# A layered kernel with two mixtures of experts: the second mixture's rows are sorted sequence by sequence, in groups of five and three

## The chip, the cores and the metric

The kernel runs on one core of a Trainium2 chip. The metric is device time in microseconds (us). Five engines work side by side, each through its own queue in order: PE multiplies matrices, DVE and ACT do elementwise work, POOL does some of it and issues the indirect DMAs, SP issues the other DMAs. PE weight loads appear as a track of their own, PEld.

## The reference, cut to what matters

```python
# x: 8 sequences of 512 rows of 128, float32
x = x + 0.5 * moe(layernorm(x))        # layer 0: 8 experts, top 2, 128 -> 512 -> 128
x = x + attention(layernorm(x))        # layer 1: 16 heads of 8, causal, with rope
x = x + 0.5 * moe(layernorm(x))        # layer 2: same weights as layer 0
x = x + 0.5 * fp6_linear(layernorm(x)) # block quantized, block 32
x = x + mix(layernorm(x))              # rmsnorm, gates, causal scan, gated MLP
x = x + 0.5 * fp6_linear(layernorm(x))

def moe(u):
    logits = u @ router_w + router_b
    gates, idx = top_2(logits); gates = softmax(gates)
    return sum(gates[k] * (relu(u @ W1[idx[k]] + b1[idx[k]]) @ W2[idx[k]] + b2[idx[k]]) for k in (0, 1))
```

## The kernel before, in words

The eight sequences X[b] stay in SBUF, four blocks of 128 rows each. A mixture layer works in two groups of sequences (`GROUPS`; layer 0: three and five, layer 2, the third layer, four and four). For each group there are three stages.

`moe_front` (L336) routes. Each sequence, once the layer before has finished it (`done`), is normalized and scored. When all of the group are scored, one set of operations over all its rows finds the two experts of each row (`first_of_max`), counts rows by expert with two matrix products (L435, L436), and computes each row's place in a table in which every expert starts at a multiple of 256 rows. Then 8 indirect DMAs per sequence (L496) scatter the normalized rows into `rows_in[g]` in DRAM, one generator step each.

`moe_tiles` (L505) takes the table in tiles of 256 rows, `tiles_of(n)` = 4n + 7 for n sequences. `load` reads the tile's expert number into a register of SP (L514), and loads that expert's weights `wx` (L516) and the rows `xs` (L520); the latter depends on every scatter of the group. `rows_turned` transposes the rows (L530), `first` does the first product (L544) and the relu (L552, L554), `second` the second (L564), adds a bias (L572) and stores into `rows_out` (L576). `ahead` loads five tiles ahead and turns up to two ahead, as soon as the loads are emitted. A tile takes four generator steps. The loop emits `first(i, half)` and then `second(i - 1, half)`, so the end of a tile is emitted after the start of the next one.

`moe_combine` (L608) gathers the two result rows of every row (L636, 8 indirect DMAs per sequence on POOL) and adds them to X with the gates (L627). The first sequence is finished after 14 gathers.

All code is emitted in program order by generators. `drive(main, (side, rate), ...)` takes `rate` steps of each side per step of the main one; so the order of work on every engine's queue is the order of these steps, and the rates set what stands between what. `attention` (L652) takes 10 steps before its loop over t and then two for every t; it works through the sequences in order and finishes sequence b with L836. `tails` (L1041) runs the last three layers of the sequences, each 27 steps (`fp6`, `mix`, `fp6`), a new one every 8 steps, at most four at once. The end of the order reads:

```python
drive(
    attention(list(range(nb)), 1),
    (early, 1.0), (tiles, 2.2), (gathering, 0.8), (third, 1.0), (fourth, 1.0), (beside, 0.9),
)
finish(third)
drive(until(beside, lambda: filled(2, 0)), (fourth, 1.5))
rest = tails(GROUPS[2][0] + GROUPS[2][1])
drive(beside, (fourth, 1.5), (moe_combine(2, 0), 1.0), (rest, 0.33))
drive(rest, (moe_combine(2, 1), 2.0))
```

Here `third` and `fourth` route the groups of layer 2, `beside` is its tiles, `sent(s, g)` is true once the group's scatters are all emitted, `filled(s, g)` once its tiles' stores are. `early`, `tiles` and `gathering` are what is left of layer 0.

Of the kernel before, what the change touches and what calls it, by code (L numbers as in the profile page):

```python
# [25 lines left out]
NGF = 3  # L26
TW = 256

GROUPS = {0: [[0, 1, 2], [3, 4, 5, 6, 7]], 2: [[0, 1, 2, 3], [4, 5, 6, 7]]}
SIZES = sorted({len(g) for gs in GROUPS.values() for g in gs})  # L30
GTX = SIZES[-1] * NT


def tiles_of(n):

    return 2 * n * S // TW + NE - 1
# [7 lines left out]

NWIDE = 12
KBUFS = 5
AHEAD = 4


# [15 lines left out]
def drive(main, *sides):  # L65

    due = [0.0] * len(sides)
    for _ in main:
        for i, (g, rate) in enumerate(sides):
            due[i] += rate  # L70
            while due[i] >= 1.0:
                due[i] -= 1.0
                next(g, None)
# [12 lines left out]
def kernel(  # L86
# [71 lines left out]
        rows_in.append(dram.tile([n, P], F32, tag=f"rows_in{g}", name=f"rows_in{g}"))  # L158
        rows_out.append(dram.tile([n, P], F32, tag=f"rows_out{g}", name=f"rows_out{g}"))

    def clear_rows(g):
        n = rows_in[g].shape[0]
        nc.sync.dma_start(
            out=rows_in[g].rearrange("(n p) c -> p n c", p=P),
            in_=zero.unsqueeze(1).to_broadcast([P, n // P, P]),
        )

    for b in range(3, nb):
        load_x(b)
# [65 lines left out]
    def power(v, eps, name):  # L235
        rs = small.tile([P, NT], F32, tag="rs", name=f"rs_{name}")
        nc.vector.tensor_scalar_add(rs, v, eps)  # L237
        nc.gpsimd.tensor_tensor(rs, rs, mhalf[:, 0:NT], ALU.pow)  # L238
        return rs

    def moments(src, name, mv=None):
        st = small.tile([P, NT, nc.vector.BN_STATS_DIM], F32, tag="bst", name=f"st_{name}")
        if mv is None:
            mv = small.tile([P, NT, nc.vector.BN_AGGR_DIM], F32, tag="bmv", name=f"mv_{name}")
        for t in range(NT):
            nc.vector.bn_stats(out=st[:, t, :], in_=src[:, t, :])  # L246
        for t in range(NT):
            nc.vector.bn_aggr(out=mv[:, t, :], in_=st[:, t, :])
        return mv

    def normed_act(src, mv, rs, name, tag="u"):

        nb_ = small.tile([P, NT], F32, tag="nbias", name=f"nb_{tag}_{name}")
        nc.vector.scalar_tensor_tensor(nb_, mv[:, :, 0], -1.0, rs, ALU.mult, ALU.mult)  # L254
        u = wk.tile([P, NT, P], F32, tag=tag, name=f"{tag}_{name}", bufs={"um": 5, "row": 4}.get(tag, 2))
        for t in range(NT):
            nc.scalar.activation(  # L257
                u[:, t, :], src[:, t, :], AF.Identity,
                scale=rs[:, t : t + 1], bias=nb_[:, t : t + 1],
            )  # L260
        return u

    def normed(src, mv, rs, name):

        u = wk.tile([P, NT, P], F32, tag="um", name=f"um_{name}", bufs=5)
        for t in range(NT):
            nc.vector.tensor_scalar(
                u[:, t, :], src[:, t, :], mv[:, t, 0:1], rs[:, t : t + 1],
                ALU.subtract, ALU.mult,
            )  # L270
        return u

    def by_feature(src, name, scale=None, tag="uT"):

        tp = turned(src, name)
        ut = wk.tile([P, S], F32, tag=tag, name=f"uT_{name}")
        if scale is None:
            nc.scalar.copy(ut, tp)
        else:
            nc.scalar.activation(ut, tp, AF.Copy, scale=scale)  # L280
        return ut
# [35 lines left out]
        return ins  # L317

    def filled(s, g):
        return len(groups[s, g]["stored"]) == tiles_of(len(GROUPS[s][g]))  # L320

    def sent(s, g):
        return (s, g) in groups and len(groups[s, g]["scattered"]) == 2 * NT * len(GROUPS[s][g])

    groups = {}
    fronts = {}
    done = set()
    backlog = []
# [7 lines left out]
    def moe_front(s, g):  # L336
# [149 lines left out]
        nc.vector.tensor_tensor(g1[:, 1, :], ex, g1[:, 0, :], ALU.mult)  # L486
        yield

        scattered = []
        groups[s, g] = dict(at=at, gates=g1, eid=eid, scattered=scattered, stored=[])  # L490
        yield
        for n in range(len(bs)):
            for k in range(2):
                for t in range(NT):
# [7 lines left out]
                    scattered.append(unordered(ins, f"out{name}"))  # L502
                    yield

    def moe_tiles(s):  # L505

        order = [(g, i) for g in range(2) for i in range(tiles_of(len(GROUPS[s][g])))]
# [2 lines left out]
        def load(at):  # L510
            g, i = order[at]
            name = f"{s}_{g}_{i}"
            state = groups[s, g]
            e = nc.sync.value_load(state["eid"][0:1, i : i + 1], min_val=0, max_val=NE - 1)  # L514
            wx = wide(f"wx_{name}")
            nc.sync.dma_start(  # L516
                out=wx, in_=wexp[bass.ds(e, 1), :, :].rearrange("o p c -> p (o c)")
            )
            xs = wk.tile([P, 2, P], F32, tag="xs", name=f"xs_{name}", bufs=4)
            ins = nc.sync.dma_start(  # L520
                out=xs, in_=rows_in[g][ts(i, TW), :].rearrange("(h p) c -> p h c", p=P)
            )
            data_from(ins, state["scattered"])
            T[at] = dict(wx=wx, xs=xs, name=name, to=(g, i))

        def rows_turned(i):
            t = T[i]
# [51 lines left out]
            del T[i]  # L579

        n = len(order)
        loaded = turns = 0

        def ahead(i, turn):

            nonlocal loaded, turns
            while loaded < min(i + AHEAD + 1, n) and sent(s, order[loaded][0]):
                load(loaded)
                loaded += 1
            while turn and turns < min(i + 3, loaded):  # L590
                rows_turned(turns)
                turns += 1

        for i in range(n + 1):
            for half in range(2):
                if i < n:
                    ahead(i, turns <= i)
                    while turns <= i:
                        yield
                        ahead(i, True)  # L600
                    first(i, half)
                    ahead(i, half == 1)
                yield
                if i >= 1:
                    second(i - 1, half)
                    yield

    def moe_combine(s, g):  # L608

# [447 lines left out]
    def behind(gen, ready):  # L1057
        while not ready():
            yield
        yield from gen  # L1060

    def until(gen, ready):
        for _ in gen:
            yield
            if ready():
                return

    for s in GROUPS:
        for g in range(2):
            fronts[s, g] = moe_front(s, g)  # L1070
    first_front, second_front = fronts[0, 0], fronts[0, 1]
    next(first_front)
    next(second_front)
# [12 lines left out]
    )  # L1086
    backlog += [early, tiles, late]
    gathering = behind(late, lambda: filled(0, 1))
    third, fourth = fronts[2, 0], behind(fronts[2, 1], lambda: sent(2, 0))
    more_tiles = moe_tiles(2)  # L1090
    beside = behind(more_tiles, lambda: sent(2, 0))
    drive(
        attention(list(range(nb)), 1),
        (early, 1.0), (tiles, 2.2), (gathering, 0.8), (third, 1.0), (fourth, 1.0), (beside, 0.9),
    )
    finish(third)
    drive(until(beside, lambda: filled(2, 0)), (fourth, 1.5))
    rest = tails(GROUPS[2][0] + GROUPS[2][1])
    drive(beside, (fourth, 1.5), (moe_combine(2, 0), 1.0), (rest, 0.33))
    drive(rest, (moe_combine(2, 1), 2.0))  # L1100


# [75 lines left out]
```

## Time and profile before

| | us |
|---|---|
| median of 3 runs (1143.15 to 1146.67) | 1144.25 |
| the profiled execution, its own time | 1143.83 |
| its span | 1142.1 |
| PE busy | 947.7 (83%) |
| DVE busy | 674.8 (59%) |
| POOL busy | 539.0 (47%) |
| ACT busy | 485.0 (42%) |
| first L836 (a sequence leaves attention), last | 340.7, 715.8 |
| scatters of group 0 of layer 2 end; of group 1 | 607, 778 |
| last tile's L572 | 926.6 |
| gathers of group 0 of layer 2 begin; of group 1 | 795.9, 930.1 |

The span is the time between the first and the last instruction of the profiled execution; its own time is 1.7 us more. Busy times of the engines overlap. The page also cuts the span in 40 slices and gives the busy share of each; the trace can be asked for the busy times in any stretch, the instructions in order of time, and what each waited for (in square brackets: the idle time before it and what ended it).

### The profile page before, as it was taken

The numbers are of one execution on the slowest core, as the hardware profiler recorded it, in microseconds if no ns is written. First come the engines' busy times: TensorE is split into PE (matmuls) and PEld (weight loads), VectorE is DVE, ScalarE is ACT, GpSimd is POOL, SyncE is SP. The second block draws the span as 40 slices with busy tenths as digits, with TensorE's granted clock in tenths as the row PEclk, the third lists the DMA queues.
The fourth block names the chain that finished last, engine by engine and source line by source line (L and its number), as shares of the span: only waits on it lengthen the run. The fifth ranks groups of instructions, "written<-read, shape, count | busy, mean of one in ns | idle before, by whom it ended". The sixth has DMA issues, their size and how long they took to land.

```text
span 1142.1 us, 20198 instructions
## 1 busy us (share of the span) xinstructions
PE 947.7 (83%) x6681; PEld 651.5 (57%) x6681; DVE 674.8 (59%) x2484; ACT 485.0 (42%) x1063; POOL 539.0 (47%) x694
## 2 busy tenths in 40 slices
PE   3569989999999999999994999985779975367773
PEld 2459987777644445454442666875767753234432
DVE  7323244555688888779863641621566676877763
ACT  1323323324555566665552554321245444244441
POOL 3778063002487754433893221172852258754431
PEclk9999999999999999999997999997889986677787
DMA  9579776442110000000014213575655111000000
GB/s 294 176 243 276 227 219 190 148 126 68 29 27 24 25 13 1 1 2 2 29 57 144 60 62 95 160 224 175 200 173 173 47 33 41 23 19 10 10 10 18
DMA packets 88312, 110.05 MB, mean 96 GB/s; under 512 B 9360, under 2 KB 69648, under 8 KB 88208
## 3 DMA queue, kind: packets, MB, share of 16 engines
q1 hardware_dynamic: 80016, 91.97, 26.4%
q0 software_dynamic: 8192, 16.79, 4.9%
q8 instruction: 53, 0.87, 0.3%
q14 instruction: 51, 0.42, 0.1%
HBM read 79.63 MB, written 29.10 MB: 95 GB/s over the span
## 4 chain that ended last, share of the span: by engine, by line
PE 58%; DVE 16%; POOL 9%; issue 9%; ACT 4%; DMA 4%; SPq 0%; POOLq 0%; DVEq 0%; ACTq 0%
PE sa L731 11%; PE yp L564 10%; PE hp L544 10%; PE av L796 6%; PE sb L731 4%; POOL rows_in L496 3%; POOL y L636 3%; DVE seen L748 2%; DVE st L246 2%; ACT um L257 2%; PE lp L350 1%; PE gt L1015 1%; PE up L1016 1%; PE tp L231 1%; DMA xs<-rows_in 1%
## 5 line engine op out<-in xcount | busy, mean ns | idle before, releaser
L748 DVE CUSTOM_DVE_ANT_0 seen<-sa,future_s 128x128 f32<-128x128 f32 (+3 forms) x512 | 225.8, 487 | 91.6 <-PE sb L731 73.6
L777 ACT ACTIVATE pm<-sb 128x512 f32<-128x512 f32 (+1 forms) x384 | 180.5, 523 | 150.6 <-PE sb L731 138.8
L552 ACT ACTIVATE hs<-hp,wx 128x256 f32<-128x256 f32 x276 | 119.7, 470 | 255.3 <-PE hp L544 180.0
L731 PE MATMUL sb<-qa,ka 32*128 32x384 f32 (+3 forms) x1024 | 216.2, 468 | 0.7 <-DVE nstat L748 0.7
L564 PE MATMUL yp<-wx,hs 128*128 128x128 f32 x1472 | 202.9, 282 | 4.6 <-ACT hs L552 4.0
L564 PEld LDWEIGHTS yp<-wx,hs 128*128 128x128 f32 x1472 | 190.9, 197 | 19.0 <-issue 7.9
L544 PE MATMUL hp<-xt,wx 128*128 128x256 f32 x736 | 199.1, 395 | 0.0
L731 PE MATMUL sa<-ka,qz 32*128 32x256 f32 (+3 forms) x1024 | 197.2, 466 | 1.8 <-issue 1.6
L782 POOL TENSOR_SCALAR_AFFINE_SELECT pm<-pm 128x256 f32<-128x256 f32 x256 | 101.8, 411 | 191.2 <-ACT pm L777 190.3
L636 POOL DMA_INDIRECT y<-rows_out,at x128 | 131.9, 1030 | 85.8 <-DMA rows_out<-yo 50.4
L554 DVE TENSOR_SCALAR hs<-hp,wx 128x256 f32<-128x256 f32 x92 | 44.4, 483 | 171.8 <-ACT hs L552 161.9
L544 PEld LDWEIGHTS hp<-xt,wx 128*128 128x128 f32 x736 | 131.8, 198 | 24.3 <-issue 5.5
L731 PEld LDWEIGHTS sa<-ka,qz 32*128 32x128 f32 x1024 | 94.5, 184 | 75.0 <-issue 28.6
L731 PEld LDWEIGHTS sb<-qa,ka 32*128 32x128 f32 x1024 | 103.1, 184 | 16.0 <-DVE nstat L748 4.3
L496 POOL DMA_INDIRECT rows_in<-um,at x88 | 86.8, 986 | 45.8 <-DVE q L467 23.9
L796 PE MATMUL av<-pm,vpad 128*32 128x512 f32 (+3 forms) x1024 | 88.8, 442 | 2.6 <-DVE nstat L748 1.6
L238 POOL TENSOR_TENSOR rs<-rs,mhalf 128x4 f32<-128x4 f32 x35 | 36.2, 1033 | 87.6 <-DVE rs L237 87.5
L530 PE MATMUL xp<-cst,xs 128*128 128x128 f32 x184 | 37.3, 287 | 44.6 <-DMA xs<-rows_in 44.6
L231 PE MATMUL tp_xd<-cst,q 128*128 128x128 f32 x64 | 14.6, 370 | 63.8 <-POOL q L918 63.8
L257 ACT ACTIVATE um<-x,nb_um,rs 128x128 f32<-128x128 f32 x96 | 39.5, 482 | 63.5 <-DVE nb_um L254 55.5
L796 PEld LDWEIGHTS av<-pm,vpad 128*32 128x32 f32 x1024 | 23.5, 108 | 73.6 <-issue 43.9
L627 DVE SCALAR_TENSOR_TENSOR x<-y,g,x 128x128 f32<-128x128 f32 x128 | 54.0, 424 | 12.4 <-DMA y<-rows_out,at 10.2
(190 smaller groups left out, 1274.4 us busy)
## 6 DMA issues: line engine op xcount, KB each, us to landing
wx<-in_wexp SPq DMA_DIRECT2D x92, 578.0 KB, 3.9
xs<-rows_in SPq DMA_DIRECT2D x92, 128.0 KB, 4.1
rows_out<-yo SPq DMA_DIRECT2D x92, 128.0 KB, 1.9
rows_in<-zero SPq DMA_DIRECT2D x1, 3456.0 KB
rows_in<-zero SPq DMA_DIRECT2D x1, 2944.0 KB
x<-in_x SPq DMA_DIRECT2D x8, 256.0 KB, 5.4
y<-rows_out,at POOLq DMA_INDIRECT x128
out_x<-x SPq DMA_DIRECT2D x8, 256.0 KB, 2.0
```

Source lines behind the costliest of these rows:

```text
L257: nc.scalar.activation(u[:, t, :], src[:, t, :], AF.Identity, scale=rs[:, t : t + 1], bias=nb_[:, t : t + 1],)
L496: ins = nc.gpsimd.indirect_dma_start(out=rows_in[g][0 : NTL * TW, :], out_offset=bass.IndirectOffsetOnAxis(ap=at[:, k, i : i + 1], axis=0) ...
L544: nc.tensor.matmul(hp[:, k, :], wx[:, E_W1 + fc * P : E_W1 + (fc + 1) * P], t["xt"], start=True, stop=True,)
L552: nc.scalar.activation(hs[:, fc, :], hp[:, k, :], AF.Relu, bias=bias)
L564: nc.tensor.matmul(yp[:, h, :], t["hs"][:, fc, ts(h, P)], wx[:, E_W2 + fc * P : E_W2 + (fc + 1) * P], start=(fc == 0), stop=(fc == NFC - 1),)
L627: nc.vector.scalar_tensor_tensor(X[b][:, t, :], y[:, k, :], gates[:, k, i : i + 1], X[b][:, t, :], ALU.mult, ALU.add,)
L636: ins = nc.gpsimd.indirect_dma_start(out=y[:, k, :], out_offset=None, in_=rows_out[g][0 : NTL * TW, :], in_offset=bass.IndirectOffsetOnAxi ...
L731: nc.tensor.matmul(sc[:, at : at + hi - lo], stat[rows, ts(m, P)], mov[rows, lo:hi], start=True, stop=stop,)
L748: nc.vector.tensor_tensor_reduce(out=seen(w), in0=sc[:, at : at + w], in1=future_s[:, S - w : S], scale=-1.0, scalar=3.0e38, op0=ALU.add, ...
L777: nc.scalar.activation(pm[:, h % 2, 0:w], sc[:, 0:w], AF.Exp, scale=scale)
L782: nc.gpsimd.affine_select(out=dg, in_=dg, pattern=[[0, 2], [1, P]], compare_op=ALU.is_ge, fill=0.0, base=0, channel_multiplier=-1,)
L796: nc.tensor.matmul(av[32 * j : 32 * j + 32, m * P :], Q[b]["v"][:, m * NH + NR * j + r, :], U[n]["pms"][p, j // 2][:, j % 2, at : at + S - ...
```

## The change

For layer 2 `moe_stream` replaces `moe_front`. Each expert gets a stretch of a new table (`by_stretch`) that is long enough for all rows of the group, so that a sequence's places need only the counts of the sequences before it (`end`). Each sequence is routed by itself when attention has finished it, and its rows are scattered at once: with a generator step per scatter, but for the group's last sequence, whose eight scatters are emitted together. Where the tiles lie is known at the end; the first row of each is computed into `row`, and `load` reads it into a second register of SP for the address of `xs`. The places of the results in `rows_out` are then computed by adding `move`; `placed` tells that this has been done. The new tables are cleared beside attention by 16 DMAs. A tile's rows are turned `LANDING` = 6 steps after their load at the earliest. The groups of layer 2 are of five and three sequences (27 and 19 tiles; 23 and 23 before), and the rates of the order are others. `um` tiles have four buffers instead of five, and `rows_in[0]` has 27 tiles instead of 23.

```diff
-GROUPS = {0: [[0, 1, 2], [3, 4, 5, 6, 7]], 2: [[0, 1, 2, 3], [4, 5, 6, 7]]}
+GROUPS = {0: [[0, 1, 2], [3, 4, 5, 6, 7]], 2: [[0, 1, 2, 3, 4], [5, 6, 7]]}
...
+LANDING = 6
...
+    stretch = [len(bs) * S for bs in GROUPS[2]]
+    by_stretch = [
+        dram.tile([NE * n, P], F32, tag=f"by_stretch{g}", name=f"by_stretch{g}")
+        for g, n in enumerate(stretch)
+    ]
+
+    def clear_stretches():
+        for g, n in enumerate(stretch):
+            for e in range(NE):
+                cleared(by_stretch[g][ts(e, n), :])
+                yield
...
     def filled(s, g):
-        return len(groups[s, g]["stored"]) == tiles_of(len(GROUPS[s][g]))
+        return (s, g) in placed and len(groups[s, g]["stored"]) == tiles_of(len(GROUPS[s][g]))
...
+    def moe_stream(s, g):
...
+        for n, b in enumerate(bs):
+            while (s - 1, b) not in done:
+                yield
+            sl = ts(n, NT)
+            mv = moments(X[b], f"{s}_{b}")
+            rs = power(mv[:, :, 1], 1e-5, f"{s}_{b}")
+            yield
+            yield
+            yield
+            u = normed_act(X[b], mv, rs, f"{s}_{b}", tag="um")
...
+            lp = bank(f"lp_{s}_{b}")
+            for t in range(NT):
+                nc.tensor.matmul(lp[:, ts(t, NE)], ut[:, ts(t, P)], rw_s, start=True, stop=True)
+            yield
...
+            for k in range(2):
+                m = small_tile(f"m{k}", n, (NT, 1))
+                nc.vector.tensor_reduce(m, l, AX.X, ALU.max)
+                is_max = small_tile("k", n)
+                nc.vector.tensor_tensor(is_max, l, m.to_broadcast([P, NT, NE]), ALU.is_equal)
+                yield
...
+            nc.tensor.matmul(in_tile, before, by_expert, start=True, stop=True)
+            nc.tensor.matmul(
+                of_tile.rearrange("p (e t) -> p e t", e=NE), ones, by_expert, start=True, stop=True
+            )
+            yield
...
+            nc.vector.tensor_tensor(
+                place, place, end.unsqueeze(2).to_broadcast([P, NE, NT]), ALU.add
+            )
...
+            nc.vector.tensor_tensor(new_end, end, inc[:, :, NT - 1], ALU.add)
+            end = new_end
+            yield
+            for k in range(2):
+                for t in range(NT):
+                    ins = nc.gpsimd.indirect_dma_start(
+                        out=table,
+                        out_offset=bass.IndirectOffsetOnAxis(ap=at[:, k, t : t + 1], axis=0),
+                        in_=u[:, t, :], in_offset=None,
+                        bounds_check=NE * cap - 1, oob_is_err=False,
+                    )
+                    scattered.append(unordered(ins, f"out{name}"))
+                    if n < len(bs) - 1:
+                        yield
...
+        groups[s, g] = dict(
+            at=at, gates=g1, eid=eid, row=row, table=table, scattered=scattered, stored=[]
+        )
+        yield
...
+        placed.add((s, g))
...
-            ins = nc.sync.dma_start(
-                out=xs, in_=rows_in[g][ts(i, TW), :].rearrange("(h p) c -> p h c", p=P)
-            )
+            if "row" in state:
+                r = nc.sync.value_load(
+                    state["row"][0:1, i : i + 1], min_val=0, max_val=NE * stretch[g] - TW
+                )
+                rows = state["table"][bass.ds(r, TW), :]
+            else:
+                rows = rows_in[g][ts(i, TW), :]
+            ins = nc.sync.dma_start(out=xs, in_=rows.rearrange("(h p) c -> p h c", p=P))
             data_from(ins, state["scattered"])
-            T[at] = dict(wx=wx, xs=xs, name=name, to=(g, i))
+            T[at] = dict(wx=wx, xs=xs, name=name, to=(g, i), since=steps)
...
-            while turn and turns < min(i + 3, loaded):
+            while turn and turns < min(i + 3, loaded) and steps >= T[turns]["since"] + LANDING:
                 rows_turned(turns)
                 turns += 1
...
-            fronts[s, g] = moe_front(s, g)
+            fronts[s, g] = (moe_front if s == 0 else moe_stream)(s, g)
...
-    third, fourth = fronts[2, 0], behind(fronts[2, 1], lambda: sent(2, 0))
+    third, fourth = fronts[2, 0], behind(fronts[2, 1], lambda: (2, 0) in placed)
     more_tiles = moe_tiles(2)
     beside = behind(more_tiles, lambda: sent(2, 0))
+    back = behind(moe_combine(2, 0), lambda: filled(2, 0))
     drive(
         attention(list(range(nb)), 1),
-        (early, 1.0), (tiles, 2.2), (gathering, 0.8), (third, 1.0), (fourth, 1.0), (beside, 0.9),
+        (early, 1.0), (tiles, 2.2), (gathering, 0.8), (clear_stretches(), 0.2),
+        (third, 1.5), (fourth, 1.5), (beside, 2.0), (back, 0.8),
     )
     finish(third)
-    drive(until(beside, lambda: filled(2, 0)), (fourth, 1.5))
+    drive(until(beside, lambda: filled(2, 0)), (fourth, 2.0))
     rest = tails(GROUPS[2][0] + GROUPS[2][1])
-    drive(beside, (fourth, 1.5), (moe_combine(2, 0), 1.0), (rest, 0.33))
+    drive(beside, (fourth, 2.0), (back, 1.0), (rest, 0.6))
     drive(rest, (moe_combine(2, 1), 2.0))
```

## The prediction

> **What bounds the kernel now.** I read the page's slices first, then the busy time by stretch, then the chain that ended last, and last the instructions around the two largest holes of PE.
>
> ```profile
> PE   3569989999999999999994999985779975367773
> DVE  7323244555688888779863641621566676877763
> ```
>
> A digit is 28.6 us. PE (counting slices from 0) is full from slice 6 to 26 but for slice 21, near 610 us; it dips at slice 27, from 771 us, and from slice 32 (914 us) on it is not full again. So three places matter to this change: two holes, and the end.
>
> ```profile
> 600.00:625.00 25.00, 10.59 (x70) 5.39 (x68) 7.76 (x39) 4.89 (x12) 9.57 (x14) 0.66 0.50 164
> ...
> 766.00:783.00 17.00, 0.49 (x3) 0.52 (x4) 0.48 (x1) 0.18 (x1) 9.84 (x11) 0.58 0.19 55
> 783.00:817.00 34.00, 33.34 (x221) 30.53 (x220) 13.39 (x43) 9.18 (x21) 15.62 (x16) 0.96 0.83 249
> 817.00:927.00 110.00, 93.33 (x554) 78.34 (x555) 69.45 (x224) 53.42 (x122) 46.12 (x44) 0.92 0.40 118
> 927.00:1006.00 79.00, 43.56 (x167) 26.30 (x166) 56.99 (x169) 27.07 (x60) 59.29 (x56) 0.74 0.13 35
> 1006.00:1070.00 64.00, 44.75 (x160) 28.32 (x159) 46.34 (x150) 30.21 (x66) 28.54 (x26) 0.71 0.03 10
> 1070.00:1142.00 72.00, 39.66 (x173) 24.82 (x172) 40.78 (x116) 22.29 (x47) 21.85 (x20) 0.78 0.04 15
> ```
>
> Columns: stretch, its length, busy us of PE, PEld, DVE, ACT, POOL, then PE's clock, DMA share, GB/s. PE loses 14.4 us in the first row and 16.5 in the second. From 817 to 927 (tiles of group 1 with the first tails) PE is 85% busy: that stretch is PE's. From 927 (tails alone) no engine is over 76%: chains of short steps set it, 215 us long.
>
> ```profile
> 611.65 0.66 PE L530 MATMUL xp<-cst,xs 128*128 128x128 f32 x2 [9.00 <-DMA xs<-rows_in]
> 782.51 0.66 PE L530 MATMUL xp<-cst,xs 128*128 128x128 f32 x2 [16.84 <-DMA xs<-rows_in]
> 715.80 0.68 DVE L836 TENSOR_TENSOR x<-x,y 128x512 f32<-128x512 f32 x1
> 738.25 1.07 POOL L496 DMA_INDIRECT rows_in<-um,at  x1 [19.30 <-DVE q L467]
> 777.91 0.97 POOL L496 DMA_INDIRECT rows_in<-um,at  x1 [0.30 <-issue]
> ```
>
> Both holes are the same wait: the transpose of a group's first tile needs rows whose scatter has just ended. The last three rows give the second one: attention ends at 715.8, routing takes 22.4 us, 32 scatters 1.28 us apart take 40.6, and PE goes on at 783.2.
>
> [...]the last scatter lands 2.26 us after its issue (the chain's DMA row at 777.91), and SP issues xs at 780.30. [...]here L514's TENSOR_LOAD has a median of 273 ns, so I use that. [...]L352, of that size, takes 180 to 193.
>
> **When things happen in the new order.** I count yields. Attention has 10 before its loop and 2 per t; sequence b is done at yield 24b+57. DVE's L836 puts b=4 at 544.9, b=5 at 592.0, b=6 at 668.4, b=7 at 715.8: 47.1 us per 24 yields without tiles, 1.96 each. A tile in the dense stretch costs PE 3.73 us (L572 every 3.73). Taking the stall and 3.6 tiles (13.4) out of yields 177 to 201 leaves 48.7 us, and 5.4 tiles (20.1) out of 201 to 225 leaves 27.2.
>
> *Group 0 sent.* Sequence 4 is done at yield 153; 15 steps at rate 1.5 put its 8 scatters at yield 163 (564.5 us) and `sent` at 165. Eight scatters by 1.28 make 10.2, landing 2.3, xs 5.4 (the chain's row at 612.8): rows in at 582.4. LANDING lets the transpose go at yield 168, where PE arrives at 574: a stall of 8 instead of 14.4. The burst also sits ahead of the affine selects on POOL; I take that wait as inside the 8 (0 to 4 outside).
>
> *Attention's end.* Two tile steps per yield from 168 make 108 by yield 222, all 27 first halves. So 26.5 tiles lie inside attention where 9.3 do now. 582.4 + 17.6 + 48.7 + 27.2 + 26.5 x 3.73 (98.8) = 774.7, and 3 for the stream's waits (below): 778.
>
> *The new hole.* No tile is left to hide what follows. Routing of sequence 7 uncovered, from the rows at 715.8 to 723: 7.4 us to the logits, then 22 DVE operations of about 0.2 with two PE products between, together 14.7. Eight scatters 9.9, landing 2.3, load and transpose 3.2: 30 us, so group 1's first tile turns at 808, against 783.2. By balance: 5.25 tiles more are done by then (24.75 remain now, 19.5 after), 19.6 us; holes 38 instead of 31.4; and the 3: 812. I take 808.
>
> *Combine.* `filled(2,0)` needs the second half of tile 26, which the loop emits after the first half of tile 27, so after group 1 is sent. `back` at 0.8 inside attention therefore gathers nothing. The first tail starts 28 us after the turn today (811.1); now only half a tile, not three, stands before the last store: 23. First tail at 831.
>
> **The mixed stretch.** Today 90 tile yields remain, 14 pass before the first sequence is combined, 76 x 0.33 = 25 steps of tails; the trace shows 27 at 927 (step 28, the first tail's last sum, is at 929.5). After: 74 - 14 = 60, x 0.6 = 36 steps. PE work per step of one live tail: busy 221 us from 817 on, less 17 tiles (63), over 216 live steps = 0.74. Today 2.80 of tiles per step: 8 steps with one live, 8 with two, 8 with three, 3 with four = 118 against 116 measured, so PE sets it. After, 1.55 of tiles per step: 8 x 2.29 + 8 x 3.03 + 8 x 3.77 + 12 x 4.51 = 127. In-order PE waits for POOL's L918 in a tail's first stages: 10.4 us for 5 quantizations in 817:927, 37.4 for 8 in 927:1070. Fewer tile yields between the steps leave less cover: 7 at 3.4, midway, are 24, 13 more: 140. Last tile at 971 (now 927).
>
> **The tails alone.** 51.5 steps instead of 60: sequence 5's gathers start with step 36, 14 of them at 2 per step, its tail at 43.5, then two intervals of 8 and 28 steps. Prices by the same phases today (L950 at 929.5, 966.5, 1006.2, 1034.0, 1069.9, 1093.8, 1117.4, 1138.0): with gathers 4.8 per step, then 3.3, at the end 3.0, 2.95, 2.6. 12 x 4.8 + 4 x 3.3 + 8 x 3.2 + 11.5 x 3.0 + 8 x 2.95 + 8 x 2.6 = 175, against 211. Plus 4 for the store.
>
> **Sum.** 808 + 23 + 140 + 175 + 4 = 1150 of span, against 783 + 28 + 116 + 211 + 4 = 1142.1. The profiled execution took 1143.83, 1.7 over its span and 0.4 under the median of 1144.25: **1152 us**. In short: a shorter routing is paid for by losing its cover, and four tiles moved early are PE work either way.
>
> **Parts costed at little.** The stream's DVE work: 22 operations by 0.19 are 4.2 us per sequence, today about 25 by 0.28 per group, 1.8 per sequence; 2.4 more on a DVE 78% busy in 425:600 beside PE at 98%. PE waits for `both` at L435: 7.2 us on two occasions today; per sequence 0 to 3.6, I take 0.4, so 3. Clearing the stretches: 16.8 MB in 16 DMAs, 1.3 and 0.8 MB, one per 5 yields; at 270 GB/s (SP sits 11.06 us behind today's clear of 3.0 MB) 5 us at most for one. Behind them stand layer 0's tile loads, sent four tiles ahead, over 20 us: nothing, 5 if that cover fails. rows_in of group 0 grows by 0.5 MB, 2 us before a first scatter at 26: nothing. The second register load adds 0.5 us per tile to SP, under PE's 3.73. One um buffer less: tails hold one each, at most four live: 0 to 5. Gathers and scatters stay 64 each on POOL.
>
> **Rivals.** *Faster, about 1131.* The tails fill the tiles' gaps without further waits: the mixed stretch is 127, not 140, and with five sequences combined early POOL stops setting the 12 steps with gathers, 4.1 instead of 4.8 (-8): 1152 - 13 - 8 = 1131. For it: DVE and POOL are under 65% in 817:927. Against: the 37.4 us of waits at L918 once tiles are scarce. It decides at a last tile before about 960. *Clearly slower, about 1176.* Every sequence's routing stops PE in attention by the 3.6 us seen at L435: 7 x 3.2 more = 22, and 2 for the burst on POOL. For it: one DVE queue serves attention's maxima and these chains. Against: rate 1.5 leaves most of a yield between producer and consumer. It decides at attention ending after 795. *It doesn't do what it says:* LANDING is too short and the first hole stays 14.4: +6, inside the forecast's band.
>
> **Chances.** Forecast's band, 1141 to 1163: 0.45 (0.12 of it within 0.3% of 1144.25, that is 1141 to 1148, about what a measurement can tell; the rest above). Faster 0.36, clearly slower 0.19. So faster 0.36, same 0.12, slower 0.52. Range: down to 1118 (rival one with attention hiding 10 us more) and up to 1176; about 1 in 10 is left out on either side.[...]
>
> **What would show it.** Right: the hole near 580 is 6 to 10 us; L836 ends near 778; PE then idles about 27 us before an xs load; the first gather comes after that; the last L572 is near 970; 3 sequences gather after it. Wrong: gathers inside attention; a hole under 15 us after it; a last tile before 960; or attention ending after 795.

## The result: 5% slower, and the profile after

| | before | after |
|---|---|---|
| median | 1145.46 us (4 runs, 1143.15 to 1147.98) | 1202.33 us (4 runs, 1201.40 to 1203.42) |
| ratio | | 1.0496, 95% interval 1.0470 to 1.0523 |
| span of the profiled execution | 1142.1 | 1201.7 |
| sequence 0 leaves attention | 340.7 | 340.9 |
| sequence 4 | 544.9 | 577.4 |
| sequence 7 | 715.8 | 814.0 |
| first tile of group 1 turned | 783.2 | 843.6 |
| last tile's end | 926.6 | 1026.0 |

The forecast was 1152 us, its range 1118 to 1176: the sign was right, the size was not. All times are in us from the start of the span. The slices of the page after answer to those shown of before (a digit is 30.0 us).

```profile
PE   3479989999988999999979999992757878546774
PEclk9999999999997989898889999995778988767776
```

The first hole, at slice 20, has become smaller, as it should. The second, at slice 27, is still there. New is what PEclk, the granted clock of PE in tenths of full speed, shows in slices 12 to 19: digits of 7 and 8 among the nines, where PE is 80% busy or more. In the kernel before, these slices are all 9 (the page of `z_before` below shows them).

Next the busy time by stretch, with the columns as in the prediction: the first hole, the second one, the gathers after it, tiles with tails, tails alone.

```profile
600.00:625.00 25.00, 16.75 (x129) 7.38 (x122) 20.03 (x72) 7.12 (x16) 13.33 (x19) 0.84 0.41 123
...
814.00:844.00 30.00, 5.22 (x18) 3.73 (x18) 11.75 (x60) 2.44 (x6) 8.93 (x9) 0.54 0.17 48
844.00:876.00 32.00, 26.73 (x166) 24.27 (x166) 10.79 (x36) 7.41 (x17) 13.24 (x14) 0.84 0.75 227
876.00:1026.00 150.00, 111.67 (x590) 87.29 (x590) 101.14 (x306) 65.03 (x147) 73.36 (x68) 0.85 0.25 76
1026.00:1201.70 175.70, 100.86 (x377) 60.89 (x376) 112.08 (x342) 61.79 (x134) 84.75 (x79) 0.72 0.06 19
```

PE loses 8.3 us in the first row, 24.8 in the second. The instructions at both holes, in order of time:

```profile
618.26 0.41 PE L720 MATMUL xp<-cst,xs 128*128 128x128 f32 x2 [1.05 <-DMA xs<-by_stretch]
621.64 0.46 PE L720 MATMUL xp<-cst,xs 128*128 128x128 f32 x2 [2.97 <-DMA xs<-by_stretch]
624.86 0.66 PE L720 MATMUL xp<-cst,xs 128*128 128x128 f32 x2 [2.77 <-DMA xs<-by_stretch]
842.95 0.69 PE L720 MATMUL xp<-cst,xs 128*128 128x128 f32 x2 [16.70 <-DMA xs<-by_stretch]
814.01 0.69 DVE L1030 TENSOR_TENSOR x<-x,y 128x512 f32<-128x512 f32 x1 [1.84 <-PE y L1026]
837.92 0.97 POOL L621 DMA_INDIRECT by_stretch<-um,sat  x1 [0.30 <-issue]
```

L720 is the transpose of a tile's rows (L530 before), L1030 is the last step of a sequence in attention (L836), L621 a scatter (L496). In place of the one wait of 9.00 us that ended at 611.65 there are three shorter ones, 6.8 together. From the last L1030 to the last scatter it takes 24 us instead of 62, and PE still waits 16.70 for the first rows of group 1, against 16.84 before.

From the first tile of group 1 to the end the kernels take the same: 358.9 before (1142.1 - 783.2), 358.1 after. So the 60 us of span are all lost ahead of it: 32.4 between sequence 0 and sequence 4 (204.1 becomes 236.5), 28 behind that.

Where attention lost its 32.4 shows in stretches of 3 us around the routing of sequence 1:

```profile
419.00:422.00 3.00, 2.80 (x29) 1.79 (x27) 2.86 (x15) 1.95 (x4) 1.90 (x4) 1.00 0.00 0
422.00:425.00 3.00, 1.52 (x6) 0.80 (x6) 2.84 (x15) 0.76 (x2) 1.70 (x3) 0.82 0.19 42
425.00:428.00 3.00, 2.72 (x12) 0.68 (x11) 2.92 (x15) 2.57 (x8) 1.40 (x3) 0.50 0.03 7
428.00:431.00 3.00, 3.00 (x15) 1.20 (x19) 1.57 (x6) 0.30 (x1) 0.31 (x1) 0.50 0.00 0
431.00:434.00 3.00, 3.00 (x24) 0.91 (x16) 1.85 (x8) 0.79 (x2) 0.41 (x1) 0.50 0.00 0
434.00:437.00 3.00, 3.00 (x38) 1.88 (x37) 2.45 (x7) 1.97 (x4) 0.96 (x2) 0.98 0.00 0
```

PE is full in rows four and five, but executes fewer matmuls than in the last row (15 and 24 against 38): its clock is 0.50. "Half clock" below means a piece of the trace in which the granted clock is 0.50. "Clock lost" is the length of such a piece times the share that was not granted, so half its length. The instructions in the second row say what went ahead of it:

```profile
421.50 0.18 DVE L574 TENSOR_TENSOR k<-k,cst 128x32 f32<-128x32 f32 x1
421.71 0.19 DVE L576 TENSOR_REDUCE km<-k 128x4 f32<-128x32 f32 x1
421.94 0.49 DVE L577 TENSOR_TENSOR oh<-cst,km 128x32 f32<-128x32 f32 x1
422.46 0.28 DVE L580 SCALAR_TENSOR_TENSOR l<-oh,l 128x32 f32<-128x32 f32 x1
422.66 0.54 DVE L942 CUSTOM_DVE_ANT_0 seen<-sa,future_s 128x384 f32<-128x384 f32 x1
...
423.48 0.83 PE L925 MATMUL sb<-qa,ka 32*128 32x256 f32 x2 [1.67 <-DVE nstat L942]
```

A step of the routing (L574 to L580) stands on DVE's queue ahead of attention's maxima (L942). PE's next score product waits 1.67 us for those maxima; in the program all tiles in PSUM, PE's output memory, take turns in one pool of eight buffers. Then, from 423.9 to 434.1, the clock is 0.50. Between sequences 0 and 4 the trace has five pieces at half clock, 6.8 to 10.2 us long, which cost 20.5 us of full clock, and PE idles 18.0 us instead of 7.4. The two add 31.1 of the 32.4. In the kernel before there is no such piece between these sequences.

### The profile page after: what moved, and what is told of

Read it like the earlier page. It is cut to its first block, busy times and chain, and to the rows that moved or that the text cites. A ratio compares the mean times of both kernels' runs of the same rounds, so it can differ in the third digit from the quotient of the medians.

```text
span 1201.7 us, 20661 instructions
## 1 busy us (share of the span) xinstructions
PE 980.9 (82%) x6705; PEld 664.2 (55%) x6705; DVE 702.3 (58%) x2636; ACT 484.9 (40%) x1063; POOL 539.1 (45%) x694
## 5 line engine op out<-in xcount | busy, mean ns | idle before, releaser
L942 DVE CUSTOM_DVE_ANT_0 seen<-sa,future_s 128x128 f32<-128x128 f32 (+3 forms) x512 | 226.1, 487 | 119.5 <-PE sb L925 99.6
L925 PE MATMUL sb<-qa,ka 32*128 32x512 f32 (+3 forms) x1024 | 221.0, 484 | 5.9 <-DVE nstat L942 5.9
L925 PE MATMUL sa<-ka,qz 32*128 32x256 f32 (+3 forms) x1024 | 206.0, 482 | 1.8 <-issue 1.6
L734 PE MATMUL hp<-xt,wx 128*128 128x256 f32 x736 | 203.0, 401 | 0.0
L830 POOL DMA_INDIRECT y<-rows_out,at x128 | 132.5, 1035 | 88.4 <-issue 47.9
L734 PEld LDWEIGHTS hp<-xt,wx 128*128 128x128 f32 x736 | 133.6, 200 | 31.1 <-issue 8.5
L990 PE MATMUL av<-pm,vpad 128*32 128x512 f32 (+3 forms) x1024 | 98.4, 480 | 12.2 <-POOL pm L976 7.6
L621 POOL DMA_INDIRECT by_stretch<-um,sat x64 | 63.6, 994 | 30.4 <-issue 17.0
L990 PEld LDWEIGHTS av<-pm,vpad 128*32 128x32 f32 x1024 | 25.1, 114 | 91.7 <-issue 64.8
L720 PE MATMUL xp<-cst,xs 128*128 128x128 f32 x184 | 38.0, 291 | 42.0 <-DMA xs<-by_stretch 28.7
```

Of the source, the lines that this page charges most:

```text
L621: ins = nc.gpsimd.indirect_dma_start(out=table, out_offset=bass.IndirectOffsetOnAxis(ap=at[:, k, t : t + 1], axis=0), in_=u[:, t, :], in_o ...
L734: nc.tensor.matmul(hp[:, k, :], wx[:, E_W1 + fc * P : E_W1 + (fc + 1) * P], t["xt"], start=True, stop=True,)
L830: ins = nc.gpsimd.indirect_dma_start(out=y[:, k, :], out_offset=None, in_=rows_out[g][0 : NTL * TW, :], in_offset=bass.IndirectOffsetOnAxi ...
L925: nc.tensor.matmul(sc[:, at : at + hi - lo], stat[rows, ts(m, P)], mov[rows, lo:hi], start=True, stop=stop,)
L942: nc.vector.tensor_tensor_reduce(out=seen(w), in0=sc[:, at : at + w], in1=future_s[:, S - w : S], scale=-1.0, scalar=3.0e38, op0=ALU.add, ...
L990: nc.tensor.matmul(av[32 * j : 32 * j + 32, m * P :], Q[b]["v"][:, m * NH + NR * j + r, :], U[n]["pms"][p, j // 2][:, j % 2, at : at + S - ...
```

## The experiments

They ran on several chips. On some the kernel before takes 1234 to 1239 us. Of these 90 us about 60 lie ahead of the first sequence's end (near 400 instead of 340), the others behind attention: `x3_dve_only` and `x6_dve_rate1`, which change nothing there, have a turn of 87.6 instead of 67.4 and a rest of 367 to 370 instead of 360. So each ratio is to the kernel before on the same chip, and stages are measured from sequence 0's end. A ratio of a slower chip can't be set against one of a faster chip; the change as it is ran on the faster kind alone (`z_before`, `z_after`, `z_beside12` and `z_cover_again` are of that kind, all others of the slower). Attention of the kernel before's order from sequence 0 to 4 takes 204.1 and 204.2 us on the chips of the first profile and of `z_before`, and 204.2 on a slower one (`x4_landing`, which does not touch it), so lengths of this stage compare across chips. A ratio with three decimals is of a single execution; the others are of four to six, with their 95% interval in the text. In the table "0 to 4" is that stage, "lost" the clock lost in it, "4 to 7" the rest of attention, "turn" from its end to the first tile of group 1, "rest" from there to the end, all in us.

| kernel | ratio | 0 to 4 | lost | 4 to 7 | turn | rest |
|---|---|---|---|---|---|---|
| x1_rate1 | 1.006 | 213.0 | 3.4 | 232.9 | 29.0 | 363.2 |
| x2_clear_early | 1.050 | 232.8 | 15.4 | 235.7 | 29.7 | 363.1 |
| x3_dve_only | 1.014 | 218.8 | 10.2 | 175.1 | 87.6 | 370.0 |
| x6_dve_rate1 | 1.006 | 214.8 | 1.7 | 172.9 | 87.6 | 366.7 |
| x4_landing | 0.9882 | 204.2 | 0 | 151.8 | 92.9 | 365.9 |
| x8_cover | 0.9801 | 211.5 | 0 | 186.3 | 48.1 | 361.8 |
| z_before | 1.001 | 204.2 | 0 | 176.0 | 67.4 | 360.4 |
| z_after | 1.0474 | 235.9 | 20.5 | 236.4 | 29.8 | 358.1 |
| z_beside12 | 1.0159 | 236.0 | 20.5 | 196.3 | 38.1 | 355.8 |
| z_cover_again | 0.9916 | 213.5 | 3.4 | 181.3 | 45.7 | 353.9 |
| w_no_scatter | 1.016 | 222.9 | 13.7 | 236.1 | 29.6 | 363.5 |
| w_dve_pe | 1.025 | 225.2 | 15.4 | 181.9 | 87.8 | 370.0 |

### Which part of the change stops PE in attention?

**The routing's rate.** At 1.5, two routing steps fall into every second yield of attention.

```diff
-        (third, 1.5), (fourth, 1.5), (beside, 2.0), (back, 0.8),
+        (third, 1.0), (fourth, 1.0), (beside, 2.0), (back, 0.8),
```

> The changed kernel with the two routing generators at rate 1.0 beside attention, as in the kernel before, not 1.5. Theory A (routing's small DVE operations bunch up ahead of attention's maxima, PE waits for PSUM banks, its clock halves): thinner steps give most of it back; sequence 4 leaves attention at 550 to 562 us (577.4 in the changed kernel, 544.9 before), and the half-clock pieces between 300 and 580 us fall from 7 to at most 3. Theory B (the clears' 16.8 MB of DMA) and theory C (scatters on POOL stand ahead of the affine selects): the amounts are the same, 573 to 580. Total 1180 to 1200 if A, 1200 to 1206 if not.

0 to 4 fell to 213.0, with one piece at half clock; the 550 to 562 named for sequence 4 are 209 to 221 from sequence 0's end. The rate is thus worth 23 of the 32 us: as many steps and instructions, spread one per yield. The totals named can't be judged on this slower chip.

**The clearing of the stretches**, moved ahead of attention:

```diff
-        (early, 1.0), (fp6_weight(), 0.2),
+        (early, 1.0), (fp6_weight(), 0.2), (clear_stretches(), 1.0),
...
-        (early, 1.0), (tiles, 2.2), (gathering, 0.8), (clear_stretches(), 0.2),
+        (early, 1.0), (tiles, 2.2), (gathering, 0.8),
```

> The changed kernel with the 16 clears moved from attention to the stretch of layer 0's last tiles (about 143 to 178 us). Theory B: without them beside attention sequence 0 leaves its routing sooner and sequence 4 leaves attention at 560 or earlier, measured from attention's first maxima. Theories A and C: sequence 4 leaves attention as late, the same 236 us after sequence 0 (577.4 - 340.9), within 4 us; attention itself may begin up to 15 us later because the clears stand before tile loads on SP.

0 to 4 is 232.8, 3 less than with the clears in it, and from sequence 0's end to the end it takes 861.2, against 860.8 in the changed kernel. The clears are not the cause. The ratio of 1.050 says little here: with the clears ahead of it sequence 0 leaves attention at 433.7, against 402.0 in `x1_rate1` on the same chip, twice the delay that was allowed for.

**DVE's work alone.** The kernel before, with 21 operations of 128x32 per sequence in the steps of the routing; they wait for nothing and nobody waits for them.

```diff
+    def extra_dve():
+        sc = cpool.tile([P, 32], F32, tag="scratch", name="scratch")
+        for b in range(7):
+            while (1, b) not in done:
+                yield
+            for _ in range(7):
+                yield
+            for n in (2, 4, 2, 3, 2, 0, 4, 4):
+                for _ in range(n):
+                    nc.vector.tensor_tensor(sc, ones[:, 0:32], zero[:, 0:32], ALU.add)
+                yield
...
-        (early, 1.0), (tiles, 2.2), (gathering, 0.8), (third, 1.0), (fourth, 1.0), (beside, 0.9),
+        (early, 1.0), (tiles, 2.2), (gathering, 0.8), (third, 1.0), (fourth, 1.0), (beside, 0.9), (extra_dve(), 1.5),
```

> The kernel before, and beside attention, for each of the sequences 0 to 6 once it has left attention, 21 DVE operations of 128x32 on a scratch tile, in the 8 steps and at the rate 1.5 of the new routing: its DVE load alone, with no PE product, no scatter and no wait on another engine. Output unchanged. Theory A in its plain form (DVE time alone is enough): sequence 4 leaves attention 20 us or more after 544.9 and the clock halves once per sequence. Theory A2 (it needs the waits between DVE and PE), B and C: below 5 us later, no half clock between 300 and 580 us.

The same at a rate of 1.0 (`(extra_dve(), 1.0)`):

> The kernel before with the same 21 scratch DVE operations per sequence as at rate 1.5 (where attention took 14.6 us more from sequence 0 to 4), now at rate 1.0. Theory A (bunching): at most 6 us more, 204 to 210 us from sequence 0 to 4, and fewer half-clock pieces than five. Rival (DVE's time as such, 4 us per sequence, is what counts): again 12 to 17 us more, since the work is the same.

At 1.5 it costs 14.6 us over the 204.2 of before, 10.2 of them clock, in four pieces; that lies between what the theories named (20 or more, and under 5). At 1.0 it still costs 10.6, again between the two named (under 6, and 12 to 17), with 1.7 of clock lost. So the 21 operations have a price of about 2.7 us per sequence even at one step per yield, and bunching adds a part to it. What this price consists of is open: lost clock and added idle time of PE account for 6.2 of the 10.6, the other 4.4 stand as PE busy, and the ends of matmuls are modelled. The stand-in is also no exact measure of the routing's own vector work: at the same rate of 1.0 the whole routing, with its products and scatters, costs less (213.0, 8.8 more than before).

**Products and scatters.** DVE's work alone costs 14.6 of the 32. Two parts are left to try: the routing's two products on PE between the vector operations, and the scatters on POOL. The first were added to `x3_dve_only`, the second taken from the changed kernel for sequences 0 to 3, whose results of that layer are thus left out.

```diff
+                if n == 0:
+                    pt = bank(f"px_{b}")
+                    nc.tensor.matmul(pt[:, 0:32], before, sc, start=True, stop=True)
+                    nc.tensor.matmul(pt[:, 32:64], ones, sc, start=True, stop=True)
```

> The kernel before with 21 added vector operations per sequence at 1.5 steps per yield, as in x3_dve_only, and with two products of 32 columns on PE between them, which read the last of these operations, take a PSUM bank, and are read by the next one. Theory (products and banks on PE): sequence 0 to 4 rises from 218.8 to 228 to 237. Rival (scatters on POOL, or ACT's part): it stays within 217 to 222.

```diff
+                    if n == len(bs) - 1 or g == 1:
                         ins = nc.gpsimd.indirect_dma_start(
```

> The changed kernel without the 32 scatters of sequences 0 to 3 of layer 2; their rows stay zero in the table, so their results of that layer are left out. Their generator steps stay. Theory (POOL's burst of scatters holds back attention's affine selects): sequence 0 to 4 falls from 236 to 218 to 224, and the half clock after sequence 0 at its second piece goes; the wait of PE for POOL's affine select falls from 7.3 us to under 3. Rival (the products of the routing on PE and their banks): it stays at 232 to 237, with 15 to 21 us of clock lost.

Neither was the whole. The products bring 0 to 4 to 225.2, 6.4 us over `x3_dve_only` (5.2 of them clock lost), between the range named for them (228 to 237) and that of the rival (217 to 222). The scatters are worth 13.0 against `z_after`, in the range named, and 9.9 against `x2_clear_early`; 8.0 of the 13.0 lie in sequence 0 alone (65.2 to 57.2). The waits of PE between sequence 0 and sequence 4 (us in total, times, longest) show why, first in `z_after`, then in `w_no_scatter`, whose lines are one higher:

```profile
PE av L990 <- POOL pm L976: 7.3, 5, 5.0
PE sb L925 <- DVE nstat L942: 4.0, 5, 1.7
PE tp L248 <- ACT um L274: 3.0, 4, 1.1
PE av L990 <- DVE nstat L942: 2.8, 4, 1.5
```

```profile
PE av L991 <- DVE nstat L943: 3.9, 4, 1.4
PE sb L926 <- DVE nstat L943: 3.7, 4, 1.7
PE tp L248 <- ACT um L274: 2.9, 4, 1.1
```

The wait for POOL's affine selects goes, and so does the half clock at the second of the five places; the waits for DVE and ACT stay. The long one is in sequence 0, where layer 0's gathers (L830) are still on the same queue. POOL in `z_after`, in order of time:

```profile
376.44 1.04 POOL L830 DMA_INDIRECT y<-rows_out,at  x1 [0.17 <-issue]
377.79 1.01 POOL L621 DMA_INDIRECT by_stretch<-um,sat  x1 [0.30 <-issue]
379.11 0.99 POOL L621 DMA_INDIRECT by_stretch<-um,sat  x1 [0.31 <-issue]
380.09 0.44 POOL L976 TENSOR_SCALAR_AFFINE_SELECT pm<-pm 128x256 f32<-128x256 f32 x1
380.47 1.29 POOL L872 TENSOR_TENSOR ta_q<-ta_q,tb_q 128x512 f32<-128x512 f32 x1
381.92 1.01 POOL L621 DMA_INDIRECT by_stretch<-um,sat  x1 [0.17 <-issue]
382.93 0.43 POOL L976 TENSOR_SCALAR_AFFINE_SELECT pm<-pm 128x256 f32<-128x256 f32 x1
```

PE idles from 378.46 to 383.42 for the last of these. The parts add up to about the whole: 14.6 for DVE, 6.4 for the products, 10 to 13 for the scatters make 31 to 34, measured 32. That is a fair sign and no proof, since each is a single execution, the stand-in for DVE is too dear at the lower rate, and ACT's share (3.0 us of PE's waits) was not tried apart. What is shown is that the rate moves 23 of the 32 and that each of the three parts delays PE.

### What is the cover after attention worth?

The changed kernel and two rates, on one chip like that of the first profile. `z_before` and `z_after` are the two kernels as they are.

```diff
-        (third, 1.5), (fourth, 1.5), (beside, 2.0), (back, 0.8),
+        (third, 1.5), (fourth, 1.5), (beside, 1.2), (back, 0.8),
```

> The kernel before, unchanged, for a trace beside the others of this set. If the chip is the slower one of the earlier sets: about 1235, sequence 0 leaves attention near 400, sequence 4 about 204 later, no half clock between, and from sequence 0 to the end about 833; on the chip of the first profile 1144, 341, 204 and 801.

> The changed kernel, unchanged. If the ratio belongs to the change and not to the chip: 1.050 again (1.047 to 1.053) on either chip; sequence 0 to 4 takes 233 to 237, with 15 to 21 us of clock lost in 4 to 5 pieces; PE idles 21 to 25 us between the last sequence and the first tile of group 1. If the slower chip alone raises some part: a ratio outside 1.045 to 1.055.

> The changed kernel with one rate other: tiles beside attention at 1.2 steps per yield instead of 2.0; the routing stays at 1.5. Theory (bunched routing steps and lost cover are two separate costs): sequence 0 to 4 stays at 233 to 237 with the half clock, since no tile is in it; the idle time of PE after attention falls from 21 to 25 us to 4 to 6; the ratio falls by what the same rate gave at routing rate 1.0 (1.006 to 0.980, so 0.026) to 1.024 (1.018 to 1.030). Rival (the cover only works with the slower routing, because at 1.5 the group is sent earlier and the tiles run out anyway): idle stays above 15 and the ratio above 1.035. Rival (the half clock comes from the tiles' rate): sequence 0 to 4 falls below 220.

The changed kernel repeats at 1.0474 (1.0447 to 1.0501), as named. With the tiles at 1.2 per yield alone the ratio is 1.0159 (1.0126 to 1.0191), a little better than named. 0 to 4 does not move (236.0), so tiles have nothing to do with the half clock there. What moves is the place of ten tiles: 16 instead of 26 end inside attention. "4 to 7" is 40.1 shorter, "turn" only 8.3 longer. In between PE's idle time falls from 24.5 to 2.1, and the 13.6 us of clock lost there go. The slices of PE and its clock, `z_after`:

```profile
PE   3489989999988999999979999991757878545774
PEclk9999999999998989899889999995778988767776
```

and `z_beside12` (a digit is 29.2 us):

```profile
PE   3579988999999889999998999999767788545774
PEclk9999999999998889898989999999978899767776
```

The hole at slice 27 is gone; the dents in the clock from slice 12 to 20 are not. So these are two separate costs. Both rates together, first on a slower chip:

```diff
-        (third, 1.5), (fourth, 1.5), (beside, 2.0), (back, 0.8),
+        (third, 1.0), (fourth, 1.0), (beside, 1.2), (back, 0.8),
```

> The changed kernel with routing at rate 1.0 and tiles at 1.2 instead of 2.0 beside attention: some 11 of group 0's 27 tiles are left when attention ends and can stand beside the routing of sequence 7, which PE now waits out (24 us without a matmul in the changed kernel). Theory D (the lost cover costs 25 to 30 us): the hole after attention falls below 8 us and the whole kernel comes 20 to 28 us below the same with tiles at 2.0 (ratio 1.006 to the kernel before), so a ratio of 0.983 to 0.992. Rival (tiles beside attention were cheap because PE had gaps there; put behind it they cost what they fill): no gain, a ratio of 1.00 to 1.01.

> The changed kernel with routing at 1.0 and tiles beside attention at 1.2, as in x8_cover. If this chip is the slower one: 0.980 again (0.977 to 0.983). If it is the chip of the first profile: sequence 0 to the end should be 808 as in x8_cover if that stretch does not depend on the chip, against 801 before, so a ratio of 1.006; if the part after attention scales like that of the kernel before (833 to 801), 776, so 0.98.

The ratio was 0.9801 (0.9774 to 0.9828) there, a little better than named, and 0.9916 (0.9892 to 0.9940) beside the others: 1137.07 us against 1147.96 in the same set. This version beats both kernels, the kernel before by less than 1% here. From sequence 0 to the end it takes 794.5, between the two values named. Its slices (28.3 us each), and those of `z_before` (28.7):

```profile
PE   3569989999999989999999999999578788645673
PEclk9999999999999989999999999999888899667887
```

```profile
PE   3569988999999999999994999985779975467763
PEclk9999999999999999999996899997989995677787
```

Both holes of before are gone; the dip at slice 28 is the start of the tails. On the slower chip the gain was larger, and the kernel before has more to lose there, since the turn takes some 20 us longer (87.6 in `x3_dve_only` against 67.4 in `z_before`).

### The other parts

**LANDING alone**, in the kernel before: the transposes wait six steps, nothing else is changed.

```diff
-            while turn and turns < min(i + 3, loaded):
+            while turn and turns < min(i + 3, loaded) and steps >= T[turns]["since"] + LANDING:
```

> The kernel before with only the new condition that a tile's rows are turned 6 tile steps after their load at the earliest. At rate 0.9 these 6 steps are 6.7 yields of attention, 13 us, so the 14.4 us that PE loses in 600:625 should shrink below 4, and attention end 10 to 13 us sooner. Behind attention the hole of 17 us before group 1 stays, since tiles of group 0 run out at 763 either way. Total 1128 to 1136 if the hole's time is kept; 1141 to 1147 if the routing of group 1 (64 us after attention, unchanged) is all that counts and the tiles only end sooner.

0.9882 (0.9853 to 0.9911): PE's idle time from sequence 4 to 7 is 2.9 us, against 15.2 in the first profile of before, so the wait of the first hole is nearly gone. "4 to 7" is 19 to 24 us shorter than before, more than the 10 to 13 named. The hole behind attention stays: the turn is 92.9, against 87.6 in `x3_dve_only` on the same chip.

**Groups of four and four**, with the rates of the change, and then with slower ones:

```diff
-GROUPS = {0: [[0, 1, 2], [3, 4, 5, 6, 7]], 2: [[0, 1, 2, 3, 4], [5, 6, 7]]}
+GROUPS = {0: [[0, 1, 2], [3, 4, 5, 6, 7]], 2: [[0, 1, 2, 3], [4, 5, 6, 7]]}
```

> The changed kernel with groups of four and four in layer 2, all else as it is. If the five/three split is a cost or a gain of its own it shows here. Theory A (routing at rate 1.5 delays attention): sequences 1 to 4 still leave attention 230 to 238 us after sequence 0 (236.5 in the changed kernel). The split by my sum is worth nothing: four tiles more after the hole, four fewer before; the kernel stays within 10 us of the changed one relative to the kernel before, a ratio of 1.04 to 1.06. Rival: five and three let the tails start fuller, and four and four cost 15 us or more on top.

```diff
-        (third, 1.5), (fourth, 1.5), (beside, 2.0), (back, 0.8),
+        (third, 1.0), (fourth, 1.0), (beside, 0.8), (back, 0.8),
...
-    drive(beside, (fourth, 2.0), (back, 1.0), (rest, 0.6))
+    drive(beside, (fourth, 2.0), (back, 1.0), (rest, 0.33))
```

> A version for speed: the stream with groups of four and four, routing at 1.0, tiles at 0.8 beside attention so that about 8 tiles are left to cover the last sequence's routing, tails at 0.33 as in the kernel before. By the sum: both holes (14.4 and 17 us) nearly gone, attention 9 us longer for the stream: 18 to 25 us below the kernel before, a ratio of 0.979 to 0.986. If the stream's cost in attention grows beside tiles, 0.99 to 1.00.

`x5_groups44` has a ratio of 1.050, inside the 1.04 to 1.06 named, but it ran on a slower chip, so this is no comparison with the change. From sequence 0's end to the end it takes 895.7, against 860.8 in the changed kernel and 861.2 in `x2_clear_early`, which has groups of five and three and ran on a slower chip too. The rival came true: up to the turn the two agree (495.8 from sequence 0's end, 498.1 in `x2_clear_early`), but the rest takes 399.9 instead of 363.1. With tails at 0.6 the fourth sequence is through `mix` (L1225) at 1115.6, when group 1's last tile is just being finished (1117.6), and the next sequence comes to that point only 91.7 us later; in `x2_clear_early` the longest such distance is 40.8. `y1_stream44` has 0.9824 (0.9778 to 0.9870), in the range named, and can't be told from `x8_cover`, which ran on the same chip; its rest is 370.4. So four and four cost 37 us at the rates of the change and little at those of `y1_stream44`. Which of the three rates that differ there does this was not tried apart.

## Why the prediction was wrong

**The bound.** Right: the two holes, and PE from 340 to 600. The first hole lost 8.3 us, predicted 8, but in three waits and some 35 us later, so the close match is in part luck. The turn took 29.6, predicted 30, with PE idle 24.4, predicted 27. No gather fell inside attention. The tails alone took 171.6, predicted 175, and the store 4.1, predicted 4.

**The step that failed** is this one: "PE waits for `both` at L435: 7.2 us on two occasions today; per sequence 0 to 3.6, I take 0.4, so 3." Between sequences 0 and 4 alone it was 32.4. Five things were wrong in it; their costs overlap and are not to be added.
- It looked at one wait, that of the routing's product for its own input. PE waits mostly for others: attention's maxima behind the routing on DVE, attention's affine selects behind scatters on POOL. Between sequences 0 and 4 its waits for the maxima add up to 6.6 us and those for the selects to 7.6, against 1.4 and 0.9 before.
- Its upper end, 3.6 per sequence, is the mean of two waits of the kernel before, of which neither lies inside attention: one is in layer 0's routing, at the very start, and one after attention. For the one product at L435 inside attention PE did not wait at all:

```profile
21.48 0.74 PE L435 MATMUL pt<-both,cst 128*128 128x96 f32 x2 [5.49 <-DVE both L425]
522.65 0.71 PE L435 MATMUL pt<-both,cst 128*128 128x128 f32 x2
732.00 0.71 PE L435 MATMUL pt<-both,cst 128*128 128x128 f32 x2 [1.47 <-DVE both L425]
```

- The routing of the kernel before goes at one step per yield beside attention, that of the change at 1.5. Of the 32 us, 23 are that rate (`x1_rate1`), and I had named the rate as what keeps producer and consumer apart.
- DVE's added work was set at no price since DVE is 78% busy. The stand-in for it costs 10.6 at one step per yield (`x6_dve_rate1`): a queue with room on average still delays what stands behind.
- The scatters were counted as "64 each" and so as even. Before, the first one came when sequence 4 was done. Those of sequences 0 to 3 now stand between affine selects and cost 10 to 13 (`w_no_scatter`).

None of these terms had the clock in it. 20.5 of the 32 are clock lost. The pieces behind the column "lost" are 3.4, 6.8 and 10.2 us long, at 0.50. Short waits of PE go ahead of pieces here (1.67 us ahead of that of 423.9 to 434.1), but in the kernel before four waits of 1.2 to 1.4 us are followed by none (last section), so what brings the half clock on was not shown.

**The rest of the sum.** Attention from 4 to 7 took 236.6, where the sum had 230 and the 3 of the failed term. From the first tile of group 1 to the first tail were 28.4 (the first L263, at 872.1), predicted 23. The mixed stretch took 153.9, predicted 140. So the span of 1201.7 is 1150 + 32.4 - 3 + 6.6 - 0.4 + 5.4 + 13.9 - 3.4 + 0.1, to rounding. No run takes the 5.4 and the 13.9 apart, but the trace shows the clock in both. The tiles of group 1 start at half clock, which lasts from 816.4 to 854.0 and costs 5.2 us of the first stretch (1.3 in that of before). In the mixed stretch 22.2 us of clock are lost, against 8.5 before, while PE's waits for POOL's L1112, set at 24, were 16.9. The prices taken from the kernel before had its clock in them and no more. The two terms include what I had set against the loss: the tails were to give back 17 us after the turn, and that stretch came out equal. Two smaller slips changed little: the check of today's mixed stretch adds up to 120, not 118, and some 19 tiles end after 817, not 17. The 0.19 us set for each of the 22 vector operations is what L352 takes in the kernel before (an addition of two tensors of 128x32, 180 to 193 ns in 16 instances); of the routing's own, shown above, L577 took 0.49 and L580 0.28. The second register load (L706), set at 0.5 us per tile, is three instructions on SP with medians of 269, 152 and 18 ns, so 0.44.

**The rivals.** "Clearly slower" had the right queue (one DVE queue for maxima and chains) and the right point (attention's end after 795; it was 814). Its price, 22 for seven sequences and 2 for POOL, was also that of one wait without the clock, and it came to 1176, where 1202 was measured. "Faster" needed a last tile before 960; it was at 1026. The lost cover was seen ("a shorter routing is paid for by losing its cover"), but taken as given with the change. It hung on one rate of the order: 1.2 instead of 2.0 is worth 0.0315 of the ratio (`z_beside12`).

## What to carry to other kernels

Where side work is woven into a dense stretch, the rate decides as much as the amount: here one step per yield cost 9 us and one and a half cost 32, since each step delays what stands behind it on its queue (PE waited 1.67 us for maxima behind a routing step on DVE, 4.95 for an affine select behind scatters on POOL). Price such a step by who waits behind it, not by its busy time, and read the clock row beside the busy row. Work that can fill a later hole should not be hurried ahead of it: count the tiles that are left when the hole comes.

## What the runs showed of the hardware

Short waits of PE were followed by half clock in one kernel and not in another. In the 8 us ahead of the piece at 534.4 in `z_after` there is one wait, of 0.64 us, ahead of that at 421.7 one of 1.67. The kernel before (`z_before`) has four waits of 1.2 to 1.4 between sequences 0 and 4 for ACT (5.2 together) and no half clock. So the length of a wait alone does not tell when it comes. What else it needs stays open.

On the slower chips the first slices differ: the page of `x4_landing` has 155, 147, 80 and 154 GB/s in slices 1 to 4, that of `z_before` 179, 247, 280 and 226, and the first sequence leaves attention 59 us later, while attention from sequence 0 to 4 takes the same (204.2 us in both). Why these chips differ is open.
